# Two wide layers of a gated feed-forward block: from eight by eight tile products to seven products of quarters

## The chip, the core and the metric

The kernel runs on one core of a Trainium2 chip. TensorE (PE in the profile) does the matrix products, VectorE (DVE) and ScalarE (ACT) the element-wise work, GpSimd (POOL) some more of it, and it also issues the transfers that convert a number format; SyncE (SP) issues the other transfers. Each engine works through its own list of instructions strictly in the order in which the program wrote them, so an instruction that waits holds up all that stand behind it on that engine. The metric is the device time of one execution in microseconds (us), the median of three runs.

## The reference, cut to what matters

Eight sequences of 256 tokens with 256 features pass a masked causal cross attention and then a feed-forward network with two wide hidden layers of 1024.

```python
x = x + xattn(layernorm(x), ctx, ctx, mask)          # x: (8, 256, 256)
# the feed-forward part, on y = layernorm(x); einsum('bsi,oi->bso', x, w) * s is one linear layer
h = silu(lin(y, w1_w, w1_s)) * lin(y, w2_w, w2_s)    # 256 -> 1024, two layers side by side
h = gelu(lin(h, h1_w, h1_s), approximate=False)      # 1024 -> 1024, wide layer 1
h = gelu(lin(h, h2_w, h2_s), approximate=False)      # 1024 -> 1024, wide layer 2
x = x + lin(h, w3_w, w3_s)                           # 1024 -> 256
```

All weights `*_w` are drawn from -1, 0 and 1; the scales `*_s` are one number for each output feature. Results are held to single precision.

## The kernel before, in words

The 2048 tokens are worked in four blocks `t` of 512 tokens (two sequences each). Everything hidden is kept turned: a tile has 128 features on the partitions and the 512 tokens of a block along the row, so that a matrix product is 128x128 weights (stationary) against 128x512 values (moving).

**Precision.** TensorE is run in the format fp32r, which keeps fewer bits than f32. Each value is therefore split in two, `hi`, the value in fp32r (a copy on ACT), and `lo`, what is left (a subtraction on DVE, `rest`, line 221). Both parts are multiplied by the same weights and added up in PSUM. The weights fit the format as they are. While the network runs, the weights are read once more, piece by piece (`look_through`, line 163), and checked on DVE (`look`, line 159); if one doesn't fit, the whole network is done again in full f32 (`exact`), which doesn't happen with the weights of this reference.

**One block.** `feed_forward(t)` runs, for each of eight groups `o` of hidden features, `layer(w1)` into a bank `pa` and `layer(w2)` into `pb` (four 128x512 products each: two chunks of features, hi and lo), Silu on ACT, the gate on DVE, then the split. Then come the two wide layers: for each of eight outputs `o` sixteen products (eight chunks, hi and lo) into a bank `pm`, Gelu twice on ACT (once into hi, once in full for `rest`), `rest` on DVE. Last is `layer(w3)` into two banks `po`, the residual on DVE and the store.

**What is interleaved.** The attention of block `t+1` is cut into stages (`stages`, line 319). A counter of the steps of `feed_forward(t)` says behind which step one more stage is written into the lists (`STAGES`, line 537), and behind which one more piece of weights is looked at (`LOOKS`). Block 0 has its attention ahead of everything, for each of its two sequences apart. Blocks 1 to 3 read the turned queries from memory (`queries_loaded`) and turn the mean and the deviation of each token on TensorE, send them through memory and read them back as rows (`on_all`). Inputs `xs`, `kt`, `vs`, `mi` have one buffer each, so a block's inputs are loaded when the block before has done with them.

**Queues.** All weights are loaded once at the beginning from GpSimd's queue (`load_weight`, line 112): w1, w2, then h1, h2 in chunks of 512 KB, then w3. At most eight of these transfers are in flight: the ninth waits for the first, and so on. What GpSimd computes later (`mask_bias`, `yf`) stands behind them. Inputs, the pieces to be looked at and the outputs go through SyncE's queue. PSUM's eight banks are divided in four for attention (`ps_at`) and four for the products (`ps_mm`).

Of the kernel before, what the change touches and what calls it, by code (L numbers as in the profile page):

```python
# [24 lines left out]
I32 = mybir.dt.int32  # L26
AF = mybir.ActivationFunctionType
# [14 lines left out]
WARM, WARM_LATER = 11, 8  # L42
RAW = 512
# [16 lines left out]
def _network(ctx, tc, g, exact, flag):  # L60
# [13 lines left out]
    ps_at = pool("ps_at", 4, space=bass.MemoryType.PSUM)  # L74
    ps_mm = pool("ps_mm", 4, space=bass.MemoryType.PSUM)
# [48 lines left out]
    zeros = None if exact else new(work, [P, 2 * RAW], "raw", "zeros", mybir.dt.bfloat16, bufs=2)  # L124
# [8 lines left out]
    if not exact:  # L133
# [17 lines left out]
    pieces = [  # L151
        (w, r, c)
        for w in (g.w1t, g.w2t, g.h1t, g.h2t, g.w3t)
# [3 lines left out]
    seen = None if exact else new(const, [P, len(pieces)], "seen", "seen")  # L157

    def look(n, raw):
        halves16 = raw.bitcast(U16).rearrange("p (n two) -> p n two", two=2)  # L160
        nc.vector.tensor_reduce(seen[:, n : n + 1], halves16[:, :, 0], AX.X, ALU.max)  # L161

    def look_through():

        coming = []
        for n, (w, r, c) in enumerate(pieces):
            cols = min(RAW, w.shape[1] - c)
            raw = new(work, [P, RAW], "raw", f"raw_{n}", I32, bufs=2)
            nc.sync.dma_start(
                out=raw[:, :cols], in_=w[bass.ts(r, P), c : c + cols].bitcast(I32)  # L170
            )
            coming.append((n, raw[:, :cols]))
            if n:
                look(*coming.pop(0))
            yield
        look(*coming.pop())

# [23 lines left out]
    def turned(y, js, name):  # L201
# [4 lines left out]
        for c0 in range(0, ND, room):  # L206
            pt = ps_at.tile([P, room, wide], F32, tag="at", name=f"{v}{name}_{c0}")
            for c in range(room):
                for n, i in enumerate(range(NT)[tiles(js)]):
                    nc.tensor.transpose(  # L210
                        pt[:, c, bass.ts(n, P)], y[:, i, bass.ts(c0 + c, P)], ident
                    )
            pieces.append((slice(c0, c0 + room), pt))
# [31 lines left out]
    def table(t, js, func):  # L245

        if t == 0 and js == groups(t)[-1]:
            nc.scalar.activation(junk, eps, func)  # L248

# [69 lines left out]
    def stages(t, js, once, result, xs, kt, vs, mi):  # L319
        cols = tokens(js)  # L320
        queries = queries_loaded if t else queries_turned
# [88 lines left out]
        yt = [once("yth", "hyt", [P, ND, TB], dt=FR)]  # L410
        if not exact:
            yt.append(once("ytl", "lyt", [P, ND, TB], dt=FR))
        if t:
# [13 lines left out]
            for c in range(ND):  # L427
                nc.scalar.copy(yt[0][:, c, :], y[:, c, :])
                if not exact:
                    rest(yt[1][:, c, :], y[:, c, :], yt[0][:, c, :])  # L430
        else:
            y = once("y", "yf", [P, NT, D])
            normed(xs, js, mvf, y, f"f_{t}_{js[0]}")
            table(t, js, AF.Silu)
            yield
            pxt = turned(xs, js, f"pxt_{t}_{js[0]}")
            if js == groups(t)[-1]:
                keep_warm(WARM_LATER)
            yield
            for c, pt in turned(y, js, f"pyt_{t}_{js[0]}"):  # L440
                nc.scalar.copy(yt[0][:, c, cols], pt)  # L441
                if not exact:
                    rest(yt[1][:, c, cols], pt, yt[0][:, c, cols])
            yield
            for c, pt in pxt:
                nc.scalar.copy(xst[:, c, cols], pt)
        result[:] = xst, yt

    def layer(w, src, outs, name):

        pms = [ps_mm.tile([P, TB], F32, tag="mm", name=f"{v}{name}_{o}") for o in outs]
        steps = [(wc, part[:, c, :]) for part in src for c, wc in enumerate(w)]
        cut = len(w) - 1 if len(outs) > 1 else 0
        for turn_ in (range(cut), range(cut, len(steps))):
            for o, pm in zip(outs, pms):
                for n in turn_:
                    wc, x = steps[n]  # L460
                    nc.tensor.matmul(  # L461
                        pm,
                        lhsT=wc[:, bass.ts(o, P)],
                        rhs=x,
                        start=(n == 0),
                        stop=(n == len(steps) - 1),
                    )
        return pms

    PAIRS = ((0, 1), *((o,) for o in range(2, NH)))  # L470

    def feed_forward(t, xst, yt):
        hid = halves(hp, [P, NH, TB], "hid", f"ha_{t}", bufs=2)
        values = {}

        def part(o):
            value = values.pop(o)
            if not exact:
                nc.scalar.copy(hid[0][:, o, :], value)  # L479
                rest(hid[1][:, o, :], value, hid[0][:, o, :])  # L480

        for o in range(NH):
            gate = new(work, [P, TB], "tmp", f"gate_{t}_{o}", bufs=4)
            (pa,) = layer(w1, yt, (o,), f"pa_{t}")
            nc.scalar.activation(gate, pa, AF.Silu, scale=sc[:, 0, o : o + 1])  # L485
            (pb,) = layer(w2, yt, (o,), f"pb_{t}")
            values[o] = hid[0][:, o, :] if exact else gate
            nc.vector.scalar_tensor_tensor(  # L488
                values[o], pb, sc[:, 1, o : o + 1], gate, ALU.mult, ALU.mult
            )  # L490

            if o:
                part(o - 1)
            if o == NH - 1:
                part(o)
            yield
        for n, w in ((2, h1), (3, h2)):
            nxt = halves(hp, [P, NH, TB], "hid", f"h{n}_{t}", bufs=2)
            for outs in PAIRS:
                for o, pm in zip(outs, layer(w, hid, outs, f"pm{n}_{t}")):  # L500
                    scale = sc[:, n, o : o + 1]
                    nc.scalar.activation(nxt[0][:, o, :], pm, AF.Gelu, scale=scale)  # L502
                    if not exact:
                        value = new(work, [P, TB], "tmp", f"g{n}_{t}_{o}", bufs=4)
                        nc.scalar.activation(value, pm, AF.Gelu, scale=scale)  # L505
                        rest(nxt[1][:, o, :], value, nxt[0][:, o, :])
                    yield
            hid = nxt
        outs = tuple(range(ND))
        for o, po in zip(outs, layer(w3, hid, outs, f"po_{t}")):  # L510
            res = new(work, [P, TB], "tmp", f"o_{t}_{o}", bufs=4)

            last = t == NBLK - 1 and o == outs[-1]
            for a, e in ((0, S), (S, TB)) if last else ((0, TB),):
                nc.vector.scalar_tensor_tensor(
                    res[:, a:e], po[:, a:e], s3[:, o : o + 1], xst[:, o, a:e], ALU.mult, ALU.add
                )
                queue = nc.scalar if a else nc.sync
                queue.dma_start(out=g.out[bass.ts(o, P), t * TB + a : t * TB + e], in_=res[:, a:e])
            yield  # L520

    ready: list = []
    first = attention(0, ready)
# [6 lines left out]
    h1 = load_weight(g.h1t, "h1_")  # L530
    h2 = load_weight(g.h2t, "h2_")
# [3 lines left out]


    STAGES = (7, 8, 11, 12, 13, 15, 16, 17, 18, 20, 22, 23)
    LOOKS = range(NH, NH + 13)
    looking = iter(()) if exact else look_through()
    for t in range(NBLK):  # L540
        steps = feed_forward(t, *ready)
        ready = []
        ahead = iter(())
        if t + 1 < NBLK:
            loaded[t + 1] = load_block(t + 1)
            ahead = attention(t + 1, ready)
        for n, _ in enumerate(steps):
            if n in STAGES:
                next(ahead, None)
            if n in LOOKS:  # L550
                next(looking, None)
            if exact or t < NBLK - 1:
                continue
            if n == LOOKS[-1]:
                for _ in looking:
                    pass
                low = new(const, [P, 1], "low", "low")
                nc.vector.tensor_reduce(low, seen, AX.X, ALU.max)
                ones = new(const, [P, 1], "ones", "ones")
                nc.gpsimd.memset(ones, 1.0)  # L560
            if n == LOOKS[-1] + 1:
                total = ps_at.tile([1, 1], F32, tag="at", name="total")
                nc.tensor.matmul(total, lhsT=low, rhs=ones, start=True, stop=True)
                nc.vector.tensor_copy(flag, total)
            if n == 3 * NH - 2:
                more = nc.values_load(flag[0:1, 0:1], min_val=0, max_val=P * LOW)
        for _ in ahead:
            pass
    return None if exact else more
# [49 lines left out]
```

## Time and profile before

| | |
|---|---|
| median of three runs | 380.13 us (380.09 to 380.27) |
| the profiled execution: its own time, its span | 380.54 us, 378.7 us |
| TensorE busy (matmul) | 367.6 us, 97% of the span, 1618 instructions |
| VectorE busy | 177.0 us, 47%, 361 instructions |
| ScalarE busy | 179.4 us, 47%, 288 instructions |
| GpSimd busy | 51.1 us, 13%, 88 instructions |
| transfers | 36.84 MB, mean 97 GB/s; 341 to 403 GB/s from 9.5 us to 47 us |
| granted TensorE clock | 0.996 of full speed |
| table loads on ScalarE | 1283 ns each |

The span is cut into stages by what TensorE does: attention of block 0 until 21.9 us; then, for block 1, w1 and w2 from 111.6 us, the wide layers from 126.5 us to 193.2 us with the attention of block 2 between them, and w3 until 200.7 us. The other blocks look alike. Busy times of PE overlap in the records (a product's record is 400 ns long, and the next starts before it ends), so a product's cost is read from the distance of starts, not from its mean.

### The profile page before, as it was taken

The numbers are of one execution on the slowest core, as the hardware profiler recorded it, in microseconds if no ns is written. First come the engines' busy times: TensorE is split into PE (matmuls) and PEld (weight loads), VectorE is DVE, ScalarE is ACT, GpSimd is POOL, SyncE is SP. The second block draws the span as 40 slices with busy tenths as digits, with TensorE's granted clock in tenths as the row PEclk, the third lists the DMA queues.
The fourth block names the chain that finished last, engine by engine and source line by source line (L and its number), as shares of the span: only waits on it lengthen the run. The fifth ranks groups of instructions, "written<-read, shape, count | busy, mean of one in ns | idle before, by whom it ended". The sixth has DMA issues, their size and how long they took to land.

```text
span 378.7 us, 4335 instructions
## 1 busy us (share of the span) xinstructions
PE 367.6 (97%) x1618; PEld 292.9 (77%) x1619; DVE 177.0 (47%) x361; ACT 179.4 (47%) x288; POOL 51.1 (13%) x88
## 2 busy tenths in 40 slices
PE   7899999999999999999999999999999999999993
PEld 3568788888888878888888878888888888888782
DVE  4757555364246646336245745437334743222211
ACT  4476644537246562925354663543543653333320
POOL 3642350000210051000120015000030000000000
PEclk9999999999999999999999999999999999999998
DMA  6999931202119031112206313111212001110001
GB/s 194 341 403 393 374 102 57 81 29 83 57 43 289 2 96 49 52 57 83 84 2 205 128 31 103 63 57 34 78 57 78 5 2 42 42 29 0 0 5 61
DMA packets 20492, 36.84 MB, mean 97 GB/s; under 512 B 2304, under 2 KB 9264, under 8 KB 20464
## 3 DMA queue, kind: packets, MB, share of 16 engines
q1 hardware_dynamic: 15376, 22.44, 18.9%
q0 software_dynamic: 4944, 13.92, 10.7%
q8 instruction: 15, 0.25, 0.3%
q14 instruction: 13, 0.11, 0.1%
q10 hardware_dynamic: 144, 0.13, 0.1%
HBM read 34.36 MB, written 2.12 MB: 96 GB/s over the span
## 4 chain that ended last, share of the span: by engine, by line
PE 94%; DMA 1%; DVE 1%; ACT 1%; SPq 1%; issue 0%; DVEq 0%
PE pm L461 63%; PE pa L461 8%; PE po L461 8%; PE pb L461 8%; PE ps L329 3%; PE pv L388 2%; DMA kt<-ctx_t 1%; PE pxt L210 1%; PE pp L370 1%; SPq L99 0%; DVE xs L396 0%; DVE stf L182 0%; ACT L248 0%; ACT hyt L441 0%; ACT s L357 0%
## 5 line engine op out<-in xcount | busy, mean ns | idle before, releaser
L222 DVE TENSOR_TENSOR lh<-g,hh 128x512 fp32r<-128x512 f32 x64 | 45.6, 712 | 140.8 <-ACT g L505 140.8
L502 ACT ACTIVATE hh<-pm,sc 128x512 fp32r<-128x512 f32 x64 | 44.2, 690 | 137.8 <-PE pm L461 137.7
L461 PE MATMUL pm<-hh,h 128*128 128x512 f32 x256 | 66.0, 400 | 0.0
L461 PE MATMUL pm<-hha,h 128*128 128x512 f32 x256 | 65.7, 398 | 0.0
L461 PE MATMUL pm<-lh,h 128*128 128x512 f32 x256 | 64.9, 395 | 0.0
L461 PE MATMUL pm<-lha,h 128*128 128x512 f32 x256 | 64.9, 395 | 0.0
L461 PEld LDWEIGHTS pm<-lh,h 128*128 128x128 f32 x256 | 48.0, 187 | 11.7
L461 PEld LDWEIGHTS pm<-lha,h 128*128 128x128 f32 x256 | 48.0, 187 | 11.8
L461 PEld LDWEIGHTS pm<-hha,h 128*128 128x128 f32 x256 | 47.8, 188 | 11.8
L461 PEld LDWEIGHTS pm<-hh,h 128*128 128x128 f32 x256 | 47.5, 188 | 11.0
L505 ACT ACTIVATE g<-pm,sc 128x512 f32<-128x512 f32 x64 | 43.7, 683 | 0.0
L485 ACT ACTIVATE gate<-pa,sc 128x512 f32<-128x512 f32 x32 | 22.1, 690 | 35.3 <-PE pa L461 35.3
L488 DVE SCALAR_TENSOR_TENSOR gate<-pb,sc,gate 128x512 f32<-128x512 f32 x32 | 24.1, 752 | 22.3 <-PE pb L461 17.4
L161 DVE TENSOR_REDUCE seen<-raw 128x1 f32<-128x512 uint16 (+1 forms) x48 | 30.1, 628 | 0.0
L222 DVE TENSOR_TENSOR lha<-gate,hha 128x512 fp32r<-128x512 f32 x32 | 21.9, 683 | 0.4
L461 PE MATMUL pa<-hyt,w 128*128 128x512 f32 x64 | 20.2, 397 | 0.7 <-ACT hyt L441 0.7
L479 ACT CAST hha<-gate 128x512 fp32r<-128x512 f32 x32 | 19.5, 611 | 2.1 <-DVE gate L488 2.1
L461 PE MATMUL pa<-lyt,w 128*128 128x512 f32 x64 | 20.2, 397 | 0.0
L461 PE MATMUL pb<-lyt,w 128*128 128x512 f32 x64 | 20.1, 396 | 0.0
L461 PE MATMUL pb<-hyt,w 128*128 128x512 f32 x64 | 20.1, 396 | 0.0
L270 POOL DMA_DIRECT2D mf<-hmf x3 | 1.7, 582 | 117.3 <-DVE hmf L268 117.3
L502 ACT ACT_TABLE_LOAD x13 | 16.7, 1283 | 0.2
(101 smaller groups left out, 340.7 us busy)
## 6 DMA issues: line engine op xcount, KB each, us to landing
h<-h1t POOLq DMA_DIRECT2D x8, 512.0 KB, 10.3
h<-h2t POOLq DMA_DIRECT2D x8, 512.0 KB, 14.6
raw<-h1t SPq DMA_DIRECT2D x16, 256.0 KB, 2.8
raw<-h2t SPq DMA_DIRECT2D x16, 256.0 KB, 2.9
vs<-ctx_n SPq DMA_DIRECT2D x4, 512.0 KB, 7.4
out<-o SPq DMA_DIRECT2D x7, 256.0 KB, 2.7
xs<-x SPq DMA_DIRECT2D x3, 512.0 KB, 4.2
kt<-ctx_t SPq DMA_DIRECT2D x3, 512.0 KB, 6.3
```

The costliest lines, as they stand in the source:

```text
L161: nc.vector.tensor_reduce(seen[:, n : n + 1], halves16[:, :, 0], AX.X, ALU.max)
L210: nc.tensor.transpose(pt[:, c, bass.ts(n, P)], y[:, i, bass.ts(c0 + c, P)], ident)
L222: nc.vector.tensor_tensor(lo, value, hi.bitcast(F32), ALU.subtract)
L329: nc.tensor.matmul(ps[:, a:e], lhsT=qt[:, c, bass.ts(2 * j + h, P)], rhs=kt[:, c, bass.ds(j * S, e - a)], start=(c == 0), stop=(c == ND - 1),)
L370: nc.tensor.transpose(pp[:, bass.ts(k, P)], pr[:, j, bass.ts(k, P)], ident)
L388: nc.tensor.matmul(pv[:, h, :], lhsT=prt[:, j, bass.ds(a + k * P, P)], rhs=vs[:, 2 * j + k, :], start=(k == 0), stop=(k == n - 1),)
L461: nc.tensor.matmul(pm, lhsT=wc[:, bass.ts(o, P)], rhs=x, start=(n == 0), stop=(n == len(steps) - 1),)
L479: nc.scalar.copy(hid[0][:, o, :], value)
L485: nc.scalar.activation(gate, pa, AF.Silu, scale=sc[:, 0, o : o + 1])
L488: nc.vector.scalar_tensor_tensor(values[o], pb, sc[:, 1, o : o + 1], gate, ALU.mult, ALU.mult)
L502: nc.scalar.activation(nxt[0][:, o, :], pm, AF.Gelu, scale=scale)
L505: nc.scalar.activation(value, pm, AF.Gelu, scale=scale)
```

## The change

Two blocks, `t0` and `t1`, are now worked together by `pair(s, ...)`. For a wide layer the 1024 input features of both blocks are four quarters `a`, `b` (of t0) and `c`, `d` (of t1), each four tiles of 128x512, and the weights are four quarters of 512x512. Strassen's scheme in Winograd's form makes the layer from seven products of quarters instead of eight. Each product is four outputs of eight matmuls (four chunks, hi and lo). Products 1 and 2 are added up in the same banks, so are 5 and 3, and 7 and 4. Four sums of weight quarters (`S1` to `S4`) are made once by `sum_up` on DVE in bf16 and kept in device memory; the weights of each product are then loaded anew for each pair (`stationary`, three buffers). Sums of value quarters are made on GpSimd (two tiles on DVE), the results are put together by `added` on DVE, and hi and lo are made by `conv` for each product. w1, w2 and w3 stay as they were.

A pair has 80 units of eight matmuls. In the text, a layer's seven groups of four units are named after their product; their order is 1, 2, 6, 5, 3, 7, 4, and in wide layer 1 the eight w1/w2 units of t1 stand between 2 and 6. The table `plan` writes the stages of attention and the looks behind named units; the residual `xst` goes to memory (`kept`) and comes back for the end. Block 1's attention now turns its queries on the chip like block 0's (`near`), and is spread over units 0 to 13 of the first pair. The look at the wide weights tests that each is -1, 0 or 1, with two DVE instructions in place of one, 32 times, all in the second pair.

```diff
-    ps_at = pool("ps_at", 4, space=bass.MemoryType.PSUM)
-    ps_mm = pool("ps_mm", 4, space=bass.MemoryType.PSUM)
+    ps_at = pool("ps_at", 2, space=bass.MemoryType.PSUM)
+    ps_mm = pool("ps_mm", 6, space=bass.MemoryType.PSUM)
...
+        size = new(work, [P, RAW], "size", f"size_{n}", I32)
+        nc.vector.tensor_scalar(size, raw, 0x7FFFFFFF, None, ALU.bitwise_and)
+        size, n = size.bitcast(F32), n - len(small)
+        nc.vector.scalar_tensor_tensor(
+            size, raw.bitcast(F32), 0.0, size, ALU.not_equal, ALU.is_equal,
+            accum_out=count[:, n : n + 1],
+        )
...
-        queries = queries_loaded if t else queries_turned
+        queries = queries_turned if near(t) else queries_loaded
...
+        if js == groups(t)[-1]:
+            nc.sync.dma_start(out=kept(t), in_=xst)
...
+    def stationary(n, p):
...
+        a = new(wp, [P, QK, HH], "a", f"a_{n}_{p}", FR, bufs=3)
+        nc.gpsimd.dma_start(out=a, in_=src.rearrange("(k p) n -> p k n", p=P))
+        return a
...
+    def sum_loads(n, r, tags):
...
+            q = new(p, [P, 2, HH], tag, f"q{i}{j}_{n}_{r}", BF16, bufs=4)
+            src = quarter(wide_w[n], i, j)[bass.ts(r, HH // 2), :]
+            nc.gpsimd.dma_start(out=q, in_=src.rearrange("(k p) n -> p k n", p=P))
...
+    def sum_up(n, r, quarters):
+        q11, q12, q21, q22 = quarters
+        nc.vector.tensor_tensor(q22, q21, q22, ALU.add)
+        nc.vector.tensor_tensor(q21, q11, q21, ALU.subtract)
+        nc.vector.tensor_tensor(q11, q22, q11, ALU.subtract)
+        nc.vector.tensor_tensor(q12, q12, q11, ALU.subtract)
+        for there, q in zip(summed[n], (q22, q11, q21, q12)):
+            nc.sync.dma_start(out=there[...], in_=q)
...
+    def conv(value, name):
+        hi = new(hp, [P, TB], "oph", f"oh_{name}", FR, bufs=2 * QK)
+        lo = new(hp, [P, TB], "opl", f"ol_{name}", FR, bufs=2 * QK)
+        nc.scalar.copy(hi, value)
+        rest(lo, value, hi)
+        return hi, lo
+
+    def product(a, x, bank, o, steps=range(2 * QK), start=True):
+        for n in steps:
+            part, k = divmod(n, QK)
+            nc.tensor.matmul(bank, lhsT=a[:, k, bass.ts(o, P)], rhs=x[k][part], ...)
...
+            five = open_(5)
+            for o in range(QK):
+                X.setdefault(3, []).append(conv(d[o], f"{name}_3_{o}"))
+                if n == 2:
+                    nc.gpsimd.tensor_tensor(T2[o], b[o], T2[o], ALU.subtract)
+                if o == 0:
+                    fetch(base + 5)
+                product(stock[n, 5], X[5], five[o], o)
+                nd[o] = val(names["d"], f"c22_{name}_{o}")
+                added(nd[o], five[o], u[:, o, :])
+                yield
+            X.pop(5)
+            for o in range(QK):
+                X.setdefault(7, []).append(conv(c[o], f"{name}_7_{o}"))
+                if o == 0:
+                    fetch(base + 6)
+                product(stock[n, 3], X[3], five[o], o, start=False)
+                nc_[o] = val(names["c"], f"c12_{name}_{o}")
+                added(nc_[o], five[o], u[:, o, :])
+                gelu(nc_[o], nc_[o], 0, o)
+                yield
...
+    w1 = load_weight(g.w1t, "w1_")
+    w2 = load_weight(g.w2t, "w2_")
+    at_hand = {(2, p): stationary(2, p) for p in (1, 2)}
+    early = [sum_loads(2, r, [(hp, f"v{4 + r}")] * 4) for r in range(2)]
     w3 = load_weight(g.w3t, "w3_")
...
+    stages_at(1, [(0, n) for n in (0, 0, 1, 2, 4, 5, 7, 8, 9, 10, 12, 13)])
+    stages_at(2, [(0, n) for n in (14, 24, 26, 31, 33, 35, 38, 40, 41, 43, 45, 50, 52)])
+    stages_at(
+        3, [(0, n) for n in (46, 50, 52, 57, 59, 61, 64, 66, 67, 69, 71, 76)] + [(1, 9)]
+    )
+    at(0, 14, lambda: sum_up(2, 0, early[0]))
+    at(0, 17, lambda: sum_up(2, 1, early[1]))
+    for r, (load, work_) in enumerate(((28, 34), (37, 43))):
+        at(0, load, lambda r=r: late.update({r: sum_loads(3, r, [(work, "raw")] * 4)}))
+        at(0, work_, lambda r=r: sum_up(3, r, late[r]))
+    for n in range(72, 80):
+        at(0, n, lambda: next(looking, None))
+    for n in (*range(8, 16), *range(17, 43, 2), *range(44, 52), *range(53, 67, 2), 67, 68, 69, 70, 71):
+        at(1, n, lambda: next(looking, None))
```

Two groups of units (products 5 and 3) stand for the others, which are built the same way: `conv` of a later product's values, at most one sum on GpSimd, one `fetch` in the first unit, the eight matmuls, `added`, and Gelu where a result is complete.

## The prediction

> **What bounds the kernel now.** I read the chain of waits first (engines, lines, then its pieces in order of time), then the stages, then the groups.
>
> ```profile
> PE 94%; DMA 1%; DVE 1%; ACT 1%; SPq 1%; issue 0%; DVEq 0%
> 80.72 11.20 PE pm L461 x48
> 126.50:193.20 66.70, 66.70 (x302) 54.21 (x301) 32.29 (x70) 32.84 (x52) 9.14 (x14) 1.00 0.19 60
> L222 DVE TENSOR_TENSOR lh<-g,hh 128x512 fp32r<-128x512 f32 x64 | 45.6, 712 | 140.8 <-ACT g L505 140.8
> ```
>
> The chain is TensorE for 94%. 48 products take 11.20 us: 0.2333 us each. The stage row (start:end, length, busy us of PE, weight loads, DVE, ACT, POOL) shows block 1's wide layers: PE never idle, DVE and ACT half idle, POOL nearly free; DVE's 140.8 us of waiting ahead of `rest` costs nothing. So fewer products shorten the time one for one, as long as the half-idle engines can take the new work.
>
> **What it saves.** Before, 4 blocks x 2 layers x 8 outputs x 16 = 1024 wide products; after, 2 pairs x 2 layers x 7 x 4 x 8 = 896. 128 x 0.2333 = **29.9 us off**. Block 1's own turning adds 16 transposes at 0.109 (`pxt`, eight in 0.87 us) less two of 0.11: 1.5 on. PE floor: 378.7 - 29.9 + 1.5 = **350.3**. The rest asks what makes PE wait.
>
> **Start, block 1's input.** The first look at `xs_1` on DVE now stands right behind the first gate, before the second.
>
> ```profile
> 20.72 0.38 SPq L99 DMA_DIRECT2D xs<-x  x1
> DMA to landing us min/median/max: 2.1/2.4/11.7
> 26.32 0.75 DVE L488 SCALAR_TENSOR_TENSOR gate<-pb,sc,gate 128x512 f32<-128x512 f32 x1 [1.13 <-PE pb L461]
> 44.60 0.53 POOL L118 DMA_DIRECT2D w<-w3t  x1 [1.22 <-DMA h<-h2t]
> ```
>
> SP issued block 1's `xs` at 20.72; the slowest of the `xs` landings (second line: min, median, max) must be this one, the only 512 KB one issued while the weights come, so it landed at 32.4, about when the eight weight transfers then in flight (4 MB) had landed. Before, DVE touched it at 39.57. Now the store `kept` of block 0, which needs `xst` (ACT, done 22.85), stands ahead of it on SP: issue at 23.3, again behind eight transfers of 512 KB read. By read bytes it lands near 36; if the conversion to bf16, which no row shows, moves at the rate of its halved writes, near 31. I take 34.5. Then sums 4 x 0.53, gate 0.67, `rest` 0.60, reciprocal, four `ya` of 0.34, the transposes: PE goes on 5.5 us later, at 40.0. Without the wait it would get there at 21.93 + 3 x 1.87 + 0.9 = 28.4. Queued behind: ACT's Silu of unit 2 (its square root waits for the same sums), all gates on DVE. **12 us** (8 to 16). The mask bias of block 1 waits on POOL behind w3, whose last issue follows the last sum load (near 36.5), and needs 5 us: done by 42, before the scores at about 45; hidden by the first stall, and 3 to 5 us if that one is absent.
>
> **ACT's queue.** It has room (some 227 us of work by its rows) but fixed places. In layer 2 of the first pair the exponentials of block 3 stand behind unit 61, and the copies into hi for product 7 (units 62, 63) behind them: gelu 0.6, table 1.28, exponentials 2.0, copy 0.53, table 1.28, gelu 0.6, copy 0.53 ends 7.6 us after unit 61; product 7 wants that hi at 3.73 + 0.70. 3.2 us; about 0.8 more at block 1's `pv`. **4** (2 to 5).
>
> **Weights.** A load of 1 MB flows in 2.6 us (512 KB per 1.28 us between issues when alone). `S2` is finished by DVE 3 to 4 us after unit 17, stored in some 2.7 (an `out` store's landing), loaded in 6 to 7: 11 to 14.5 us after unit 17, wanted at 11.2. **1.5** (0 to 3.5). Later fetches stand two products ahead (15 us): hidden.
>
> **DVE and POOL.** This is the large term. A group of four units lasts 4 x 1.867 = 7.47 us on PE. Back to back, DVE ops come 0.60 apart (`lyt`, two in 1.28). A group holds 4 `lo` (0.60) and 4 `added` (0.61): 4.84. In the second pair come two looks a group: and-mask 0.34 to 0.60, compare 0.70, so 1.1: **7.04 of 7.47**, 6.8 in layer 2's first two groups, 9.2 in its last. That alone nearly fits. But POOL now runs 24 sums per pair in these twelve groups (and 6 earlier), and the two share something:
>
> ```profile
> 280.48 1.28 DVE L424 TENSOR_TENSOR yf<-xst,mf 128x512 f32<-128x512 f32 x2
> 283.61 1.11 DVE L222 TENSOR_TENSOR lh<-g,hh 128x512 fp32r<-128x512 f32 x1 [1.84 <-ACT g L505]
> 281.40 2.77 POOL L425 TENSOR_TENSOR yf<-yf,mf 128x512 f32<-128x512 f32 x2 [5.83 <-DVE yf L424]
> 228.32 1.11 POOL L258 TENSOR_SCALAR bias<-mi 128x128 f32<-128x128 int32 x1
> 230.06 0.64 POOL L256 TENSOR_SCALAR bias<-mi 128x128 f32<-128x128 int32 x1
> ```
>
> `lh`, 0.69 elsewhere, took 1.11 at 283.61, while POOL's second `yf` ran until 284.17; the same happened in the other two blocks. POOL's mask step took 1.11 beside a DVE subtraction and 0.64 alone. One holds up the other. The Trainium skill, *SBUF — State Buffer*, "Who interferes with whom", says that a DVE instruction with two SBUF inputs contends with a GpSimd one that reads SBUF, and that the second blocks until the first is through. By the row `lh` lost 0.43 where 0.56 of POOL's op was left; by the rule it loses all. `lo`, the looks and `sum_up` are exposed, `added` (one input in PSUM) is not. Laid end to end with 1.29 for a sum (the shortest row), and turns taken: sum, `lo`, `added` beside the next sum, and so on: the first two units of a group take DVE 7.45, the other two 3.5, so 10.95: 3.9 more a group, 0.98 a sum; some sums fall beside idle DVE, say 0.90. Second pair by the rule: 24 x 0.90 = 21.6, less DVE's room (12 x 7.47 - 85.1 = 4.5) and the 2.3 us that `lo` may be late before a product wants it: 14.8. By the row (0.05 less each) **13.5**, which I take. Ends: 0.45 a sum, 4; 1.29 a sum, 24.
>
> First pair, products 6 to 4 and layer 2's product 1: PE 51.7 (attention included), DVE 42.4 with the 8 bf16 sums of weights there at 0.60. No row shows a bf16 op[...]. *VectorE: DVE Perf Modes*, "The perf-mode tier table", gives `tensor_tensor` twice the rate in bf16; I take it since the operands are all bf16. 20 sums x 0.75 + 8 mask steps x 0.4 = 18.2, less 9.3 and 2.3: **6.6**, call it 7 (11 at the f32 row; 0 to 15 over both unknowns). POOL's transfers cost 0.55 each whether of 8 or 128 rows; that it is late itself is hidden, its sums are wanted a group later.
>
> **Sum.** 350.3 + 12 + 4 + 1.5 + 7 + 13.5 - 2 (a stall elsewhere lets DVE catch up) = 386.3. The profiled run lies 1.84 above its span, the median 0.41 below that run: 387.7, so **388 us**, 2% slower.
>
> **Rivals.** (1) *PE stays the bound*, faster: `xs_1` lands at 31 (8), POOL's sums mostly fall beside `added` and idle DVE (first pair 0, second 4), ACT 4, weights 0: 350.3 + 16 = 366.3, time **368**; up to 378 with half of the middle costs. For it: DVE's own work is below PE's in nearly every group. Against: the three collisions in the trace, and a room of only 0.43 a group. (2) *Weights late*, slower still: if converting transfers run at half rate, 1 MB takes 5 us of flow, and the first pair's loads for products 6, 7 and 4 in both layers, issued on POOL behind sums, round trips through memory and mask steps, come 2.5 late each: 15 more, **403**. For it: POOL blocks on each reused transfer slot (seen in the w3 row above). Against: h1 and h2, loaded into fp32r tiles, came at 400 GB/s. (3) *The change falls through to the full-precision network* if the new count is not exact: more than double. (4) *Costs and gain cancel*, 379.4 to 380.9.
>
> **Chances.** Forecast 0.62 (own range 381 to 398), rival 1 0.21, rival 2 0.13, rival 3 0.01, rival 4 0.03. A difference over 0.2% of 380.13 (0.76 us) can be told from none: faster 0.21, same 0.03, slower 0.76. Range 371 to 402: it cuts the fast end of rival 1 and half of rival 2.
>
> **What would show it.** In the new profile: products still 0.233 apart and 896 of them (else the floor is wrong); PE idle near 28 to 40 us behind `ya`, `xs_1` landing at 31 to 37; PE idle at product 7 of the first pair behind `oh`; in the second pair DVE busy near 100% per group, `lo` and looks well over 0.69 where POOL runs, PE waiting for `ol`. DVE durations unchanged beside POOL, or PE gapless after 45 us, would prove it wrong. If the gap at the start makes the next products come 0.43 apart, as the first warming products did, that costs 1 to 2 us more.

## The result and the profile after

The changed kernel takes **472.66 us** (median of 4 runs, 470.56 to 474.47) against 380.2 us for the kernel before on the same chip: a ratio of 1.243, 95% interval 1.237 to 1.248. The direction was forecast, the size was not: 388 us, range 371 to 402. A run that lies over 1.5% above the fastest of its kernel is left out of the times given here.

The page of the profiled execution (474.47 us, span 472.7), its busy times and its chain of waits by engine:

```profile
span 472.7 us, 4730 instructions
...
PE 380.4 (80%) x1505; PEld 288.7 (61%) x1505; DVE 324.6 (69%) x576; ACT 209.7 (44%) x352; POOL 150.7 (32%) x169
...
PE 44%; DVE 22%; issue 11%; ACT 9%; DMA 8%; POOL 1%; SPq 0%; DVEq 0%; ACTq 0%; POOLq 0%
```

TensorE was 94% of the chain and is now 44%; no engine is busy all the time. Fewer products, yet TensorE is busy for longer than the 367.6 us of before. The miss has two halves:

| | before | the forecast's sum | after |
|---|---|---|---|
| TensorE busy | 367.6 | 339.2 (367.6 - 29.9 + 1.5) | 380.4 |
| rest of the span | 11.1 | 47.1 (11.1 + 12 + 4 + 1.5 + 7 + 13.5 - 2) | 92.3 |
| span | 378.7 | 386.3 | 472.7 |
| granted TensorE clock | 0.996 | about the same | 0.907 |

45.2 us are waiting that was not foreseen, and for 41.2 us TensorE was busy longer. Most of this second part is a lower clock: in the stretches where the trace has the clock at one half, TensorE is busy for 64.0 us, which would be 32 us of work at the full clock. The other 9 us are not explained; some of it may be the records, since a product's record outlasts the step to the next product (0.40 against 0.233 us), which counts ahead of every wait. The list of waits (engine, what waited, for whom: us in total, times, longest) says where the waiting began:

```profile
ACT c L699 <- DVE c L702: 93.3, 44, 5.5
...
DVE ol L272 <- ACT oh L639: 48.1, 43, 4.5
...
PE p L648 <- ACT oh L639: 37.0, 17, 6.2
```

Line 699 is Gelu, 702 is `added`, 639 the copy into hi, 272 `rest` (lo). Gelu waits for VectorE, and VectorE waits for the hi copy, 44 and 43 times: the two engines wait for each other in turn. The timeline of one such stretch (second pair, wide layer 1, product 7; start us, length us, engine, line):

```profile
362.39 0.72 ACT L699 ACTIVATE c<-c,sc 128x512 f32<-128x512 f32 x1 [2.11 <-DVE c L702]
...
363.02 0.60 ACT L639 CAST oh<-T 128x512 fp32r<-128x512 f32 x1
363.26 1.30 POOL L804 TENSOR_TENSOR T2n<-c,T1n 128x512 f32<-128x512 f32 x1 [2.06 <-ACT c L699]
...
363.66 1.45 DVE L272 TENSOR_TENSOR ol<-T,oh 128x512 fp32r<-128x512 f32 x1 [1.30 <-ACT oh L639]
...
365.03 0.68 DVE L702 TENSOR_TENSOR c<-p,c 128x512 f32<-128x512 f32 x1
...
365.74 0.72 ACT L699 ACTIVATE c<-c,sc 128x512 f32<-128x512 f32 x1 [2.11 <-DVE c L702]
```

Read it as a ring. `lo` of the next unit needs its hi copy; that copy stands on ScalarE behind Gelu of this unit; Gelu needs `added` of this unit; `added` stands on VectorE behind `lo`. From Gelu to Gelu 3.35 us go by, for a unit of 1.87 us on TensorE. Nothing in the data asks for it: the value that hi copies was there long before. The order of the two lists makes the ring. Products 3, 7 and 4 of each layer of each pair have it: 48 units. Without a GpSimd sum in it (end of the second pair) the round took 2.6 us. Here `lo` lasts 1.45 us instead of 0.69, because a sum of GpSimd's (1.30) runs beside it.

In places VectorE waits longer:

```profile
332.77 0.78 POOL L608 DMA_DIRECT2D a<-S  x1 [6.83 <-PE p L648]
332.99 4.84 DVE L272 TENSOR_TENSOR ol<-T,oh 128x512 fp32r<-128x512 f32 x1
...
333.57 3.71 POOL L769 TENSOR_TENSOR T<-ha,T 128x512 f32<-128x512 f32 x3
...
337.89 0.80 PE L648 MATMUL p<-ol,a 128*128 128x512 f32 x1 [3.79 <-DVE ol L272]
```

This `lo` took 4.84 us: it began while GpSimd issued a weight fetch, and ended 0.55 us after the last of three sums. TensorE stood for 3.79 us. And after a long wait TensorE's products come slower:

```profile
386.48 0.79 PE L648 MATMUL p<-oh,a 128*128 128x512 f32 x1 [6.21 <-ACT oh L639]
387.07 1.91 PE L648 MATMUL p<-ol,a 128*128 128x512 f32 x4
388.77 1.91 PE L648 MATMUL p<-oh,a 128*128 128x512 f32 x4
...
391.89 1.10 PE L648 MATMUL p<-oh,a 128*128 128x512 f32 x4
```

Four products start 1.70 us from the next four, 0.43 us each, for some 5 us; then 0.233 again. The same stretch as a window (start:end, length, busy us of PE, PE loads, DVE, ACT, POOL, then granted clock, share of DMA, GB/s) has the clock at one half:

```profile
384.71:391.54 6.83, 5.07 (x12) 4.00 (x13) 4.20 (x9) 3.56 (x6) 0.00 (x0) 0.50 0.01 2
```

### The profile page after: what moved, and what is told of

Read it like the earlier page. It is cut to its first block, busy times and chain, and to the rows that moved or that the text cites. A ratio compares the mean times of both kernels' runs of the same rounds, so it can differ in the third digit from the quotient of the medians.

```text
span 472.7 us, 4730 instructions
## 1 busy us (share of the span) xinstructions
PE 380.4 (80%) x1505; PEld 288.7 (61%) x1505; DVE 324.6 (69%) x576; ACT 209.7 (44%) x352; POOL 150.7 (32%) x169
## 4 chain that ended last, share of the span: by engine, by line
PE 44%; DVE 22%; issue 11%; ACT 9%; DMA 8%; POOL 1%; SPq 0%; DVEq 0%; ACTq 0%; POOLq 0%
PE p L648 24%; DVE ol L272 9%; PE po L827 6%; PE pa L526 5%; DVE c L702 5%; ACT oh L639 4%; PE pb L526 4%; DMA xs<-x 2%; DMA ma<-hma 2%; PE ps L383 2%; PE pv L442 2%; DMA q<-h2t 2%; DMA raw<-w1t 1%; ACT s L411 1%; DVE ha L540 1%
## 5 line engine op out<-in xcount | busy, mean ns | idle before, releaser
L648 PE MATMUL p<-oh,a 128*128 128x512 f32 x448 | 139.2, 427 | 39.5 <-ACT oh L639 37.0
L648 PE MATMUL p<-ol,a 128*128 128x512 f32 x448 | 135.7, 423 | 12.9 <-DVE ol L272 12.8
L648 PEld LDWEIGHTS p<-oh,a 128*128 128x128 f32 x448 | 89.6, 202 | 68.8 <-ACT oh L639 47.9
L648 PEld LDWEIGHTS p<-ol,a 128*128 128x128 f32 x448 | 90.8, 203 | 40.0 <-DVE ol L272 18.8
L699 ACT ACTIVATE c<-c,sc 128x512 f32<-128x512 f32 x48 | 34.7, 723 | 93.5 <-DVE c L702 93.3
L272 DVE TENSOR_TENSOR ol<-c,oh 128x512 fp32r<-128x512 f32 x40 | 34.7, 870 | 24.1 <-ACT oh L639 24.0
L272 DVE TENSOR_TENSOR ol<-T,oh 128x512 fp32r<-128x512 f32 x24 | 34.9, 1470 | 11.1 <-ACT oh L639 11.1
L540 DVE SCALAR_TENSOR_TENSOR ha<-pb,sc,gate 128x512 f32<-128x512 f32 x32 | 23.5, 746 | 23.1 <-ACT gate L538 14.1
L702 DVE TENSOR_TENSOR c<-p,u 128x512 f32<-128x512 f32 x48 | 32.8, 684 | 7.6 <-PE p L648 4.1
L639 ACT CAST oh<-c 128x512 fp32r<-128x512 f32 x40 | 23.8, 609 | 17.1 <-PE p L648 9.8
L187 DVE SCALAR_TENSOR_TENSOR size<-raw,size 128x512 f32<-128x512 f32 x32 | 29.1, 909 | 1.1
L272 DVE TENSOR_TENSOR ol<-ha,oh 128x512 fp32r<-128x512 f32 x32 | 24.6, 770 | 4.2 <-ACT oh L639 4.1
L526 PE MATMUL pb<-hyt,w 128*128 128x512 f32 x64 | 20.5, 403 | 0.0
```

The costliest lines, as they stand in the source:

```text
L187: nc.vector.scalar_tensor_tensor(size, raw.bitcast(F32), 0.0, size, ALU.not_equal, ALU.is_equal, accum_out=count[:, n : n + 1],)
L272: nc.vector.tensor_tensor(lo, value, hi.bitcast(F32), ALU.subtract)
L526: nc.tensor.matmul(pm, lhsT=wc[:, bass.ts(o, P)], rhs=x, start=(n == 0), stop=(n == len(steps) - 1),)
L540: nc.vector.scalar_tensor_tensor(value, pb, sc[:, 1, o : o + 1], gate, ALU.mult, ALU.mult)
L639: nc.scalar.copy(hi, value)
L648: nc.tensor.matmul(bank, lhsT=a[:, k, bass.ts(o, P)], rhs=x[k][part], start=start and n == 0, stop=n == 2 * QK - 1, skip_group_check=not s ...
```

## The experiments

Two theories stood against each other: the **ring** (an order of instructions) and the **port** (GpSimd's sums hold VectorE up). A third was that VectorE has simply too much to do.

### Which cause: ring, port or work

**Gelu one unit later.** Each Gelu on a VectorE sum is written behind the next unit's hi copy:

```diff
                 X.setdefault(7, []).append(conv(c[o], f"{name}_7_{o}"))
+                settle()
...
                 added(nc_[o], five[o], u[:, o, :])
-                gelu(nc_[o], nc_[o], 0, o)
+                owed.append(lambda gelu=gelu, h=nc_[o], o=o: gelu(h, h, 0, o))
```

`settle` issues what is owed; products 7 and 4 are changed alike.

> Only ScalarE's order moves: in products 3, 7 and 4 each Gelu that reads a VectorE sum is issued behind the next unit's hi copy instead of ahead of it. Ring theory (lo waits for hi, hi stands behind Gelu, Gelu waits for the sum, the sum stands behind the last lo: 2.6 us round, 3.35 with a GpSimd sum in it, against 1.87 us of TensorE, in 48 units): 48 x 0.7 to 1.5 = 34 to 70 us of TensorE waiting, part of it now taken over by the GpSimd collisions: 415 to 440 us, and the wait of Gelu for the sum (93 us) and of lo for hi (48 us) mostly gone. Port theory (lo is held by GpSimd's sums, the ring only passes that on): above 460 us. The predicted terms (start 12, queue 4, weights 1.5, port 20) hold nothing for this edit: 472.

Measured: **442.91 us** (439.08 to 444.57), 29.8 less. VectorE's wait for hi fell from 48.1 to 15.7 us, TensorE's for hi from 37.0 to 7.9:

```profile
PE p L648 <- DVE ol L272: 23.5, 13, 5.6
...
DVE ol L272 <- ACT oh L639: 15.7, 11, 3.9
...
PE p L648 <- ACT oh L639: 7.9, 7, 2.1
```

The ring is real, but it is not all: this is 3 us beyond the slow end of what it expected. TensorE now waits for `lo` itself, 23.5 us instead of 12.8.

**No GpSimd sums.**

```diff
-                        T1[o - 1] = val(tags["T1"], f"T1_{name}_{o}")
-                        nc.gpsimd.tensor_tensor(T1[o - 1], c[o - 1], a[o - 1], ALU.subtract)
+                        T1[o - 1] = c[o - 1]
...
-                    nc.gpsimd.tensor_tensor(T2[o], b[o], T2[o], ALU.subtract)
```

> All of GpSimd's sums and differences of activation quarters are left out (the products then read an unsummed quarter; 4 of the 8 second-level sums a pair... those on VectorE stay). Port theory: lo is 0.69 us everywhere, and the 84 us above the forecast go almost wholly: 385 to 410 us. Ring theory: the round still takes 2.6 us in 48 units, 35 us above TensorE's own time, so 425 to 450 us, with Gelu still waiting for the sum for some 60 us or more.

Measured: **428.57 us** (427.63 to 430.18), 44.1 less for 60 sums. In the ring's range, above the port's. `lo` is 0.69 us almost everywhere, and the ring is still there: Gelu waited 82 us for VectorE.

**Both.**

> Both edits: Gelu behind the next hi copy, and GpSimd's activation sums left out. If ring and port together are the whole miss, what is left is TensorE's 350, the start (12), the queue (4), the weights (1.5) and small change: 368 to 385 us, TensorE clock back above 0.97. If it stays above 400 us a third cause of over 20 us is open (round trips through memory of the mean rows, looks waiting for their data, weights).

Measured: **400.74 us** (400.14 to 401.22), 71.9 less, close to 29.8 + 44.1 = 73.9: two causes that add up. The profiled runs, side by side (us):

| | TensorE busy | rest of the span | span |
|---|---|---|---|
| changed kernel | 380.4 | 92.3 | 472.7 |
| Gelu later | 368.1 | 72.2 | 440.3 |
| no GpSimd sums | 363.3 | 62.6 | 425.9 |
| both | 354.2 | 44.2 | 398.4 |

So the ring is worth 18 to 20 us of waiting and 9 to 12 us of longer busy time, the sums 28 to 30 and 14 to 17, each with the other in or out.

The time misses the expected 368 to 385 by 16 us, and the clock (0.958) the expected 0.97, so a third cause was open. The busy row of this run, and from its chain of waits one piece in the second pair (start us, length us):

```profile
PE 354.2 (89%) x1504; PEld 277.0 (70%) x1505; DVE 279.3 (70%) x576; ACT 208.8 (52%) x352; POOL 67.9 (17%) x109
...
294.56 73.32 PE p L648 x313
```

313 products without a gap, 0.2342 us each: in the second pair TensorE is the bound again. What is left lies in the first pair, where these waits of TensorE remain:

```profile
PE pqt L260 <- DVE ya L242: 10.7, 1, 10.7
PE p L648 <- DVE ol L272: 4.9, 2, 4.1
PE pxt L260 <- DVE hmf L322: 2.9, 1, 2.9
PE ps L383 <- issue: 2.7, 1, 2.7
PE pxt L260 <- ACT xst L500: 2.6, 1, 2.6
PE p L648 <- DMA a<-S: 2.2, 1, 2.2
PE po L829 <- DVE ol_po L272: 2.0, 1, 2.0
PE p L648 <- ACT oh L639: 2.0, 2, 1.8
```

The first is the start, with block 1's input; the second (4.1) stands behind `sum_up`, which waits on VectorE for its quarters `q` (7.34 us from issue in the chain); the three between are transposes and scores of blocks 2 and 3.

**No looks.** The operations of lines 184 and 187 are left out, the transfers stay, and the count is set to its full value.

```diff
+        if n == len(small):
+            nc.vector.memset(count, float(RAW))
+        return
         size = new(work, [P, RAW], "size", f"size_{n}", I32)
```

> The two VectorE operations of each wide look are left out (46 us of VectorE's busy time, the transfers stay; the count is set to its full value instead). If VectorE's sheer work sets the pace of the second pair, 25 to 45 us go: 428 to 447 us. Ring theory: a look stands behind the sum and ahead of the next lo, where VectorE waits for Gelu and hi (1.2 us) anyway: only 5 to 15 us go, 458 to 468 us.

Measured: **459.24 us** (458.56 to 461.67), 13.4 less for some 40 us of VectorE's busy time (324.6 to 284.6). As the ring has it: VectorE waited anyway. Its work was not the limit in this kernel.

### The port, measured by itself

Each of the two measurements here is one run, and each case in it was taken once. Behind the end of the changed kernel VectorE releases n GpSimd sums, does one sum that reads PSUM and one with both inputs in SBUF.

```diff
+    def trial(n, kind="tt", run=1, other="tt"):
+        nc.vector.tensor_copy(trig, bank)
+        for i in range(n):
+            if other == "tt":
+                nc.gpsimd.tensor_tensor(his[i % 4], trig, one, ALU.subtract)
...
+        nc.vector.tensor_tensor(mine[0], bank, two, ALU.add)
+        for i in range(run):
+            if kind == "tt":
+                nc.vector.tensor_tensor(mine[i % 4], one, two, ALU.subtract)
...
```

> The changed kernel with a measurement behind its end: a VectorE copy releases n GpSimd sums (n = 0, 1, 2, 3, 4, 6) of 128x512 f32, and VectorE does one sum that reads PSUM, then one that reads two SBUF tiles. Turns taken (the prediction's reading): the SBUF one starts when the GpSimd sum under way ends, so it takes 0.69 alone and at most 1.3 us for every n of 1 or more. Port held (what the trace of the change suggests): it waits for all sums that are queued, 0.7 + 1.3 per sum beyond the first: about 1.3, 2.6, 3.9, 5.2, 7.8 us. A sum that reads PSUM stays at 0.68 for both. With single-input or bf16 operations beside 3 sums: held as well if the port is taken by every fast mode, 0.35 to 0.7 us if only two-input f32 is affected.

Measured: 1.35 us beside one sum and 1.26 beside 2, 3, 4 and 6: **turns are taken**, as the prediction said. Each turn also costs GpSimd some 0.45 us. The case n = 3, VectorE and then GpSimd:

```profile
478.22 1.26 DVE L932 TENSOR_TENSOR b_mine<-b_one,b_two 128x512 f32<-128x512 f32 x1
```

```profile
477.67 4.15 POOL L926 TENSOR_TENSOR b_his<-b_trig,b_one 128x512 f32<-128x512 f32 x3 [0.80 <-DVE b_trig L923]
```

Four two-input operations beside four sums took 6.26 us, one of each in turn. A one-input operation went from 0.43 to 1.06, a bf16 sum from 0.41 to 1.18; sums that read PSUM stayed at 0.62 a piece. So the waits of 3.4 to 4.8 us in the changed kernel needed another reason. All of them began beside or right behind a transfer that GpSimd issued. The second measurement puts a 1 MB fetch ahead of the sums:

```diff
+        if n or dma:
+            nc.gpsimd.tensor_scalar(small_, trig[:, :1], 0.5, None, ALU.mult)
+        if dma:
...
+            nc.gpsimd.dma_start(
+                out=fill_w, in_=quarter(g.h1t, 0, 0).rearrange("(k p) n -> p k n", p=P)
+            )
+        for i in range(n):
+            nc.gpsimd.tensor_tensor(his[i % 4], trig, one, ALU.subtract)
...
```

> The changed kernel with a second measurement behind its end: as in the first, but GpSimd issues a 1 MB weight fetch ahead of its n sums, and VectorE's two-input operation begins while that issue is under way (or one or two PSUM sums later). Fetch theory: VectorE waits for the rest of the issue and all sums behind it, 0.7 + 1.25 n and some tenths: about 2.0, 3.2, 4.5 and 8 us for n = 1, 2, 3 and 6; begun after the first sum has started, it gets its turn after one sum, 1.3 to 1.9 us. Turns theory: at most 2 us for every n. Without a fetch, 3 sums: 1.26 as before. Sums that read PSUM: 0.68 in every case.

Measured, for n = 3, VectorE and then GpSimd:

```profile
489.93 4.77 DVE L939 TENSOR_TENSOR b_mine<-b_one,b_two 128x512 f32<-128x512 f32 x1
```

```profile
489.60 0.82 POOL L930 DMA_DIRECT2D b_a_tt<-h1t  x1
490.44 3.70 POOL L934 TENSOR_TENSOR b_his<-b_trig,b_one 128x512 f32<-128x512 f32 x3
```

The operation begins 0.33 us into the issue and ends 0.56 us after the third sum; with n = 6 it took 8.42. Beside three sums without the fetch, in the same run, it took 1.50 and 0.96. Behind the fetch the sums take 3.70 us instead of 4.15: no turn was given. Begun 0.56 us after the first sum it still took 3.71, which the fetch theory had wrong: the whole run of sums behind an issue is closed to VectorE. With n = 1 and 2 the operation began 0.08 us into the issue and got through in 0.69, so those two cases tell nothing of n; nor does the issue alone, without sums (0.69), where it began as early. So the length was right and the condition wider than thought.

### Is the hold on the path

**Fetches behind the sums** of their group, instead of between the first and the second:

```diff
-                if o == 0:
+                if o == 3:
                     fetch(base + 4)
```

and so for the others.

> Only the place of GpSimd's weight fetches moves: in the groups with sums it stands behind the third or fourth sum of the group instead of between the first and the second. The trace of the change has seven VectorE operations of 3.4 to 4.8 us, each begun while GpSimd issued a fetch with two or three sums queued behind it; sums without a fetch ahead of them let VectorE in after one. If the fetch ahead of queued sums is what makes VectorE wait for all of them, these seven go (7 x 2.5 to 3.5 us above a turn of 1.3 = 17 to 25 us): 448 to 458 us. If the long waits have another cause, or the later fetches come late for their product: 466 us or more.

Measured: **473.29 us** (473.01 to 474.75): no gain, outside the 448 to 458 that was expected. The time alone doesn't tell why. The waits of TensorE do:

```profile
PE p L648 <- ACT oh L639: 33.2, 19, 3.2
PE p L648 <- DMA a<-S: 21.4, 3, 9.0
```

The holds of 4.2 to 4.8 us were gone (the longest VectorE operation now took 3.3 us; the changed kernel has six of 3.4 to 4.8, not seven), but three fetches of the first pair came late by 21.4 us in all (2.2 in the changed kernel).

**The same, with those fetches of the first pair left in place.**

> As the run with later fetches (473.3), but the two fetches of each layer that came late in the first pair there (21.4 us of TensorE waiting for weights against 2.2 before) stand at their old place in that pair. If the later fetches did remove the long VectorE waits and the late weights hid it: the late weights go (19 us), the first pair's long waits partly come back (6 to 10 us): 458 to 466 us. If the long waits were never on the path: 470 us or more.

Measured: **464.43 us** (461.43 to 466.22), 8.2 less. Late weights went from 21.4 to 9.9 us only: another moved fetch of that pair, for product 7 of wide layer 1, now came 7.6 us late, though by the next group TensorE was again where it had been in the changed kernel. Three VectorE operations of 2.3 to 3.3 us were left. The hold is on the path, for at least a fifth of what the sums cost (8.2 of 44.1).

### What the clock does

Three products by a zero weight are added in each unit of the ring; they change no value.

```diff
+            for _ in range(fill if n == 0 else 0):
+                nc.tensor.matmul(bank, lhsT=none, rhs=x[k][part], start=False, stop=False, ...)
```

> The changed kernel with three products by a zero weight added in each of the 48 units of products 3, 7 and 4 (144 products, 33.6 us of TensorE at full clock), where TensorE waits. If the lower TensorE clock (0.907, busy time 380 instead of 350 us) is a consequence of the waiting: the granted clock goes to 0.95 or more and the time stays within 8 us of 472.7 or falls. If the clock falls for another reason: it stays at 0.90 to 0.91 and the time rises by 15 to 35 us.

Measured: **471.14 us** (469.31 to 473.85), clock 0.933. 144 more products cost no time, and TensorE's busy time rose by 24.4 us instead of 33.6, so the others ran faster; but 0.95 was not reached. Half a proof. More comes from five runs side by side: busy time above 339.2, beside the number of waits of 1 us or more after 25 us, is 41.2 for 25 (changed kernel), 28.9 for 17 (Gelu later), 24.1 for 18 (no sums), 15.0 for 9 (both), 36.0 for 22 (fetches later): on average 1.3 to 1.7 us of longer busy time for each wait, and 1.2 to 2.5 in the other runs. It is an average: in the changed kernel one wait of 3.6 us (until 185.1) and three of 2.0 to 2.1 us (after 428) were followed by products 0.23 us apart.

### The start, and what can be made of it

**Block 1's input early**, in a second buffer, in the kernel with both edits:

```diff
+        ahead[1] = new(io, [P, NT, D], "xs", "xs_1", bufs=2)
+        nc.sync.dma_start(
+            out=ahead[1], in_=g.x[TB : 2 * TB, :].rearrange("(i p) d -> p i d", p=P)
+        )
```

> The run with both edits (400.7) with a second buffer for a block's input, and block 1's input issued right behind block 0's, ahead of all weights. The start term says that TensorE's wait of 10.7 us at 28 to 39 us comes from this transfer alone: 389 to 393 us, gap gone. If the time of the eight weight transfers ahead of the wide layers only moves (the bus is full until 45 us), the wait comes back at w2 or at the first quarter and less than 4 us go: 397 or more.

Measured: **393.48 us** (391.75 to 393.77), 7.3 less. The wait at `ya` fell from 10.7 to 1.7 us; 2.7 us came back as a later first gate (24.6 instead of 21.9 us). This kernel has no GpSimd sum at all and still takes 13 us more than the one before.

**Sums on VectorE**, with Gelu later:

> Gelu behind the next hi copy, as in the first experiment (442.9), and all activation sums moved from GpSimd to VectorE: 52 more VectorE operations of 0.69 us, 36 us of work, none of it held by GpSimd. If what the port costs is the time in which VectorE is held (44 us in the run without the sums), doing them on VectorE itself costs about the same 36 us of work, less what falls into its idle time (first pair): 415 to 430 us. If the loss came from the sums being late on GpSimd, not from VectorE being held: below 412 us. If the two engines really overlapped most of the time: 445 us or more.

Measured: **422.24 us** (418.52 to 423.67), as the first of the three readings has it (it is 60 operations, not the 52 counted there). VectorE does for 21.5 us (over 400.7) what costs 42.2 us on GpSimd (442.9 against 400.7). With the start:

> Sums on VectorE and Gelu behind the next hi copy (422.2) with block 1's input early: the start gave 7.3 us in the kernel without sums; 412 to 416 us.

Measured: **412.29 us** (411.31 to 413.93), the fastest kernel with all work in it, ratio to the kernel before 1.082 (1.077 to 1.086). Busy times of this run by window in the second pair (columns as in the window above):

```profile
300.00:320.00 20.00, 17.34 (x72) 13.24 (x72) 19.83 (x41) 7.16 (x11) 1.48 (x2) 1.00 0.59 173
320.00:340.00 20.00, 17.63 (x73) 13.21 (x73) 19.86 (x39) 11.17 (x20) 1.48 (x2) 1.00 0.73 201
```

In these 40 us VectorE is the bound: busy for 19.8 of 20 us with its own work, TensorE for 17.5.

**Sums on GpSimd, with Gelu later, the start and fetches behind sums:**

> Three edits together, with all work left in: Gelu behind the next hi copy, block 1's input early in a second buffer, fetches behind the sums. From 442.9 (first edit alone) 7 to 11 us for the start and 12 to 20 for the fetches: 412 to 424 us. The same kernel without GpSimd's sums took 393.5, so what is above that is the price of sums whose turns VectorE and GpSimd take: the prediction had 20.5 us for it (414); held port as before: 430 us or more.

Measured: **440.21 us** (438.80 to 441.22), out of range: TensorE waited 17.1 us for weights that came late, as above. With the first pair's fetches in place:

> Gelu behind the next hi copy, block 1's input early, fetches as in the run just named. The run with the same three edits and late weights took 440.2, with 17.1 us of waiting for weights: 421 to 427 us. If it stays above 435 us, GpSimd's sums hold the path at other places than behind fetches.

Measured: **427.57 us** (425.98 to 431.90, three runs), at the slow end of the range and below the 435 that would have meant another place. Against 393.5 without sums they cost 34.1 us, turns and what is left of the hold. It is left in both pairs: in the second, one operation of a look took 7.23 us behind a fetch.

**First pair's sums on VectorE, second pair's on GpSimd:**

> As the three edits together, with the sums of the first pair on VectorE, which has room there, and those of the second pair on GpSimd with fetches behind them. If by turns a sum costs VectorE about as much as doing it (0.6 against 0.69 us), it lands beside the run with all sums on VectorE, 410 to 418 us; if turns are cheaper than that in the second pair (half of the sums beside idle time), 400 to 408.

Measured: **426.67 us** (424.13 to 427.55). Neither range: 14.4 us above the run with all sums on VectorE. At the first product of the second pair the two are level (259.0 and 258.6 us in the profiled runs), so the loss lies with the 30 sums of the second pair. But it isn't the price of turns alone. A fetch that stands behind the sums of one group stands ahead of the sums of the next, and there VectorE was held again, over five sums:

```profile
336.14 0.79 POOL L614 DMA_DIRECT2D a<-h2t  x1
...
336.53 7.22 DVE L193 SCALAR_TENSOR_TENSOR size<-raw,size 128x512 f32<-128x512 f32 x1
...
336.94 1.29 POOL L820 TENSOR_TENSOR T2n<-c,T1n 128x512 f32<-128x512 f32 x1
...
338.19 5.00 POOL L722 TENSOR_TENSOR c<-c,c 128x512 f32<-128x512 f32 x4
```

So this run does not show whether a turn is dearer than doing the sum; how much of the loss is turns, holds, lateness or slower products was not taken apart. No version ran at or below 380 us.

## Why the prediction was wrong, step by step

- **TensorE's floor**: the number and the price of the products were right, 896 of them and 0.234 us each where nothing waits. The busy time was not: 380.4 against 339.2.
- **Start, 12 us**: right. Block 1's input was issued at 23.06 (said: 23.3), landed at 33.5 (34.5); TensorE stood from 27.9 to 38.2, 10.3 us. Taking it away gave 7.3.
- **ScalarE's queue, 4**: near. 3.1 and 1.8 us of waiting behind `oh` at 218 to 224 us, where it was placed; 1.8 at that place once the ring is out. (The pieces that the prediction lists there add up to 6.8 us, not 7.6.)
- **Weights, 1.5**: right, 1.76 us at product 6 of the first pair. The cover was real but thin: fetches three units later made weights 21 us late.
- **VectorE and GpSimd, 7 + 13.5**: this step failed. The sums cost 44.1 us, 0.73 a piece, and 42.2 with the ring out: 28 to 30 us of TensorE's waiting, where 20.5 were reckoned, and 14 to 17 us of longer busy time, which the sum did not have. By pair it was 16 to 20 us in the first (said: 7) and 26 to 27 in the second (13.5). The price of a collision (0.85 to 0.90) was not too low: VectorE was busy for 0.74 to 0.79 us longer per sum. What failed is the reckoning from there to TensorE: the prediction priced 44 of the 60 sums, and took VectorE's room (9.3 and 4.5 us) and 2.3 us of slack a pair off, as if the delays spread evenly over a group. They came bunched: seven operations held behind a fetch make 23 of the 44.5 us by which VectorE was busy longer. With the ring out VectorE had idle time, and the sums still cost almost the same; why so little of it took up the delays was not taken apart. The rule that the prediction named, the Trainium skill's *SBUF — State Buffer*, "Who interferes with whom", with its exclusive lock, holds for one instruction at a time in the first measurement; behind a fetch the hold lasted over three and six sums, which neither the row nor the rule had shown (8.2 us of the time at least). The other rule, twice the rate for bf16 in *VectorE: DVE Perf Modes*, "The perf-mode tier table", held: `sum_up` took 0.69 us for 1024 bf16 elements, as `lo` does for 512 of f32, and 1.65 where GpSimd held it up.
- **"That alone nearly fits: 7.04 of 7.47"**: the same fault in its plain form, and the largest hole. Durations were added up per engine and group, and the order in which two engines wait for each other was not followed. The prediction has no term for the ring; it costs 28 to 30 us (29.8 with the sums in, 27.8 with them out). It could have been read before: in one unit, lo 0.6, `added` 0.6, Gelu 0.7 and the copy 0.6 come to 2.5 us in a closed circle, against 1.87.
- **"1 to 2 us more" for a slower clock**: right for one wait, but there were 25 waits of over 1 us. TensorE was busy for 41.2 us longer than forecast. What the clock cost of the time itself isn't known, as slower products are partly hidden behind the next wait. *TensorE: Matmul & The Clock Gate* of the Trainium skill, in "Part 1: The HAM clock gate (the "warmup" mystery)", puts half the rate behind about 3.4 us of idleness; here it stood behind waits of 1.2 to 6.2 us, and behind one of 3.6 us (until 185.1) it didn't.
- **Not in the sum**: with the ring and the sums out, the span (398.4) is still 32.6 us above the forecast without its 20.5 (365.8): 15.0 us of longer busy time and 17.6 us of waiting. Found in it are the first pair's small waits, 4.1 us behind `sum_up`'s input and 8.2 us in three waits of blocks 2 and 3, of which one, in the changed kernel, sends 4 KB of row means to memory for 10.2 us (189.04 in its chain; such stores took 1.6 to 4.0 in the kernel before).
- **Rivals**: none came in. Weights were not late, and the full-precision network was not run. The first two put the limit at one engine or one transfer; the one that happened lies between two engines.

## What to carry to other kernels

Where two engines hand values back and forth, follow the order of both lists for two units and add up the closed circle: if it is longer than the bound engine's unit, the kernel runs at the circle's pace, however idle both look. Issue the work whose input is ready (here the hi copy) ahead of the work that waits for the other engine. Don't give GpSimd sums beside a VectorE that works on SBUF, least of all behind a transfer that GpSimd itself issues (moving such a transfer behind the sums of one group puts it ahead of the next); and count the waits that a change makes, since TensorE was slower behind most of them.

## What the chip showed that was not expected

- Sums that follow a transfer's issue on GpSimd shut VectorE out until the last: 4.77 us for three, 8.42 for six, against 1.26 without the issue; 7.2 for five in a kernel. Why, no run shows.
- One-input and bf16 operations of VectorE are held as well (0.43 to 1.06 and 0.41 to 1.18 us); those with one input in PSUM are not. Beside three one-input operations of GpSimd a two-input one took 0.69 us, in one trial.
- TensorE's clock fell to one half behind most waits of 1 us or more, for 3.4 to 10.2 us at a time: 0.43 us a product.
